# Layer 0's inner product as seven block products, a planner that prefers banks already taken, the gated update split between VectorE and GpSimd, and eps as a bias

## The chip, the cores and the metric

The kernel runs on one core of a Trainium2 chip. The metric is device time in microseconds (us). The kernel before took 1354.72 us (median of three runs, 1353.41 to 1354.8). The profile below is of one more execution, which took 1352.22 us; its span, from the first to the last instruction, is 1350.3 us.

The engines are named as in the profile: PE (TensorE, matrix products), PEld (its weight loads), DVE (VectorE), ACT (ScalarE), POOL (GpSimd), SP (SyncE, which issues nearly all DMAs).

## What is computed

The input is x, 64 graphs of 256 nodes with 128 channels, and one 256 x 256 adjacency matrix A, all float32. Four layers follow one another; each adds its result to its input and normalises over the channels.

```python
x = layernorm(x + sum_k (A^k x) W_k)        # layer 0: k = 0..3, W_k of both equal adjacency chains summed
x = layernorm(x + A (x W) + b)              # layer 1
x = layernorm(x + (D A+I D) x W^T + b)      # layer 2, D = degree^-1/2
# layer 3: five gated steps, then the residual and the norm
z  = sigmoid(av W3 + h U3 + b);  r = sigmoid(av W4 + h U3 + b)   # av = [A h, A h]
hv = tanh(av W5 + (r * h) U5 + b)
h  = (1 - z) * h + z * hv
```

Layer 0 is computed as x W0' + q W2' + A (x W1' + q W3') with q = A^2 x: W0' takes in the residual's identity, the others the sums of the two chains, all with their mean over the output channels taken out, so that the result is already centred and only its variance is left to find.

## The kernel before, in words

**Groups.** The 64 graphs are worked on as 32 groups of two. Two graphs times two node blocks make a tile of 128 x 512, the size of one PSUM bank. `record` (line 732) writes down the operations of one group, from its load through all four layers to its store. At most ten groups are under way at once (ACTIVE).

**The planner.** `Plan.add` (61) stores an operation with an engine, a cost in ns, a lag, a rank and what it reads and writes; `Plan.order` (84) then simulates the engines and writes out one fixed order for each. An operation whose output has no place yet needs a free slot of its kind (8 PSUM banks; numbers of SBUF tiles on line 203). Among the operations that could start, it takes the one with the earliest possible start, and at equal starts the one of the lowest rank, which is the older group (117). The engines run in that order, waiting on semaphores. The costs and ranks are used for nothing else.

**Propagation.** `seven` (593) forms A times a group's tile: [two graphs x two node blocks] times [2 x 2 blocks of A] with seven 128-wide block products in place of eight. GpSimd forms differences of input blocks (ts01, ts2, ts3; lines 613 to 621), PE forms the products in four operations: `first` (block 0, needs no difference), `middle` (three blocks), `more` (again into block 0, after ACT has copied it away as `kept`) and `rest`; DVE and ACT put the result m together (641 to 652).

**Layer 0** (lines 736 to 788). The transposed x (xT) is made by PE for the first two groups (`near`, HEAD = 4 graphs). For the other thirty a 32 x 32 block transpose on DVE (tx, 745), a DMA to DRAM and two DMAs back bring xT with its channels permuted; its weights are therefore a permuted copy w0p, made by four DMAs (306). After q has been propagated, `first` (764) makes, for each of two node blocks, four products of 256 columns: xT and q of each graph against two weight blocks side by side. ACT copies half of each bank to v, `second` multiplies v by A into the other half, and ACT copies that to s0.

**Norm.** `spread_of` (509): ACT squares the four parts of a tile and accumulates the sums; GpSimd adds eps (519) and raises to the power -1/2 (520). `normalise_centred` (526) then scales on ACT. This is used in layers 0 to 2 of every group and at the end of the last three.

**A gated step** (813 to 835). Four 512-wide products go into bank pr (w4 m and u3 hT for r, then w34 m on top for z), two into bank ph (w5 m, u5 rh). ACT turns pr to r, then, in place, to z; and ph, in place, to hv. DVE makes rh = r hT, d = hv - hT, e = z d (into pr), hT = hT + e. `packed` (699) then transposes blocks on DVE and brings h back in node order through DRAM by DMA. The last step of the last three groups (END = 6 graphs) goes to `closing` (557) instead.

**Head.** Weights and A are prepared in `pre` operations; `rows`, the transposes of ahat and `columns` (332 to 345) make layer 2's matrix.

Of the kernel before, what the change touches and what calls it, by code (L numbers as in the profile page):

```python
# [50 lines left out]
class Plan:  # L51
# [32 lines left out]
    def order(self):  # L84
# [14 lines left out]
        while any(ready.values()):  # L99
            best = None  # L100
            for e, waiting in ready.items():
                t0 = free.get(e, 0.0)
                pick = None
                for at, op in waiting:
                    need = {}
                    for v in placed[op]:
                        if v.slot is None:
                            need[v.kind] = need.get(v.kind, 0) + 1
                    short = False
                    for k, n in need.items():  # L110
                        if len(pool[k]) < n:
                            short = True
                            break
                        at = max(at, sorted(pool[k])[n - 1][0])
                    if short:
                        continue
                    key = (max(at, t0), op.rank, op.seq)
                    if pick is None or key < pick[0]:
                        pick = (key, op)
                if pick and (best is None or pick[0] < best[0]):  # L120
                    best = pick
            assert best, "the plan is stuck"
            (start, _, _), op = best
# [34 lines left out]
def kernel(  # L158
# [42 lines left out]
    SHAPES = {"bank": [P, 512], "x": [P, 512], "w": [P, 512], "th": [P, 384], "q": [P, P], "st": [P, Q * 6], "mv": [P, Q * 2],  # L201
              "ve": [P, Q], "rs": [P, Q]}
    slots = {"bank": BANKS, "x": ACTIVE + 3, "w": 48, "th": 10, "q": 10, "dram1": 8, "dram2": 16, "st": 12, "mv": 12, "ve": 24, "rs": 12}
# [31 lines left out]
    nc.vector.memset(half, -0.5)  # L235

# [67 lines left out]
    w0p = constant("w0p", [P, 2, C])  # L304

    def permuted():
        for r in range(4):
            nc.sync.dma_start(w0p.ap.rearrange("(j r) k c -> r j k c", r=4)[r], w0s.ap[32 * r:32 * (r + 1), 0:2, :])

    pre(1.2, "SP", 1800, permuted, [w0s], [w0p])  # L310
# [32 lines left out]
    pre(0.3, "DVE", 600, rows, [ahat, dinv], [ahat])  # L343
    pre(0.3, "PE", 4 * 110, lambda: turn(p_an, ahat), [ahat], [p_an])
# [64 lines left out]
    braw, bsum = constant("braw", [P, 6]), constant("bsum", [P, 3])  # L409
# [3 lines left out]
    pre(0.4, "DVE", 150, lambda: nc.vector.tensor_add(bsum.ap, braw.ap[:, :3], braw.ap[:, 3:]), [braw], [bsum])  # L413
    zb, rb, hb = ((bsum, bsum.ap[:, i:i + 1]) for i in range(3))
# [25 lines left out]
    class Group:  # L440
# [68 lines left out]
        def spread_of(self, tag, s):  # L509

            y, ve, rs = self.val("w", "y" + tag), self.val("ve", "ve" + tag), self.val("rs", "rs" + tag)

            def squares():
                for q in range(self.q):
                    nc.scalar.activation(nat(y)[:, q, :], nat(s)[:, q, :], AF.Square, scale=C ** -0.5,  # L515
                                         accum_out=ve.ap[:, q:q + 1])

            def scales():
                nc.gpsimd.tensor_scalar(ve.ap, ve.ap, EPS, None, op0=OP.add)  # L519
                nc.gpsimd.tensor_tensor(rs.ap, ve.ap, half[:, :self.q], op=OP.pow)  # L520

            self.act(squares, [s], [y, ve], 295 * self.q)
            self.add("POOL", 1330, 100, scales, [ve], [ve, rs])
            return y, rs
# [21 lines left out]
        def normalise(self, tag, s, mv, rs):  # L546
# [8 lines left out]
            return y  # L555

# [36 lines left out]
        def seven(self, tag, h, aTs, ins, blocks):  # L593
# [32 lines left out]
            def first():  # L626
                block(0, ins(h)[:, 0, 0], aTs.ap[:, 0, :P], True)

            def middle():
                block(2, row(ts, 0), sums.ap[:, 0, :])  # L630
                block(1, row(ts, 1), sums.ap[:, 2, :])
                block(3, row(ts, 2), sums.ap[:, 1, :])
# [21 lines left out]
            started = self.pe(pe_cost(P, 1), first, [h, aTs], [ps])  # L654
            kept = self.act(lambda: nc.scalar.copy(row(u, 1), row(ps, 0)), [ps], [u], 165)
# [3 lines left out]
            self.pe(pe_cost(P, 3), middle, [ts, sums], [ps], True, (started,))  # L659
# [59 lines left out]
        def gate_(self, name, ps, func, bias, kept=True):  # L719

            t = self.val("w", name) if kept else ps
            self.act(lambda: nc.scalar.activation(t.ap, ps.ap, func, bias=bias[1], scale=1.0),  # L722
# [9 lines left out]
        def record(self):  # L732
# [5 lines left out]
            if near:  # L738
                xT, w01 = self.copied("xT", self.transposes("x", x_)), w0s
            else:  # L740

                w01 = w0p
                turn, far = self.val("w", "tx"), self.val("dram", "dx")
                xT = self.val("w", "xT")
                self.dve(lambda: nc.vector.transpose(  # L745
                    turn.ap.rearrange("p (r b i t) -> p r b t i", r=4, t=T, i=32),
                    x_.ap.rearrange("p (b t r j) -> p r b t j", r=4, t=T, j=32)), [x_], [turn])
# [9 lines left out]
            v, s0 = self.val("w", "v"), self.val("w", "s0")  # L757
            py = []

            for t in range(T):  # L760
                p = self.val("bank", f"py0{t}")
                py.append(p)

                def first(p=p, t=t):
                    for b in range(self.nb):
                        o = p.ap[:, b * 2 * C:(b + 1) * 2 * C]
                        mm(o, (tiles if near else pairs)(xT)[:, b, t], w01.ap[:, 0:2, :], b == 0, True, shared=True)
                        mm(o, tiles(qT)[:, b, t], w0s.ap[:, 2:4, :], False, True, shared=True)

                def moved(p=p, t=t):  # L770
                    nc.scalar.copy(parts(v)[:, t], four(p)[:, :, 1, :])

                self.pe(pe_cost(2 * C, 2 * self.nb), first, [xT, qT, w01, w0s], [p])
                self.act(moved, [p], [v], 55 + 107 * self.nb)
            for t in range(T):

                def second(p=py[t], t=t):
                    for kt in range(T):
                        mm(four(p)[:, :, 0, :], aT.ap[:, kt, t * P:(t + 1) * P], parts(v)[:, kt],
                           False, True, shared=True)  # L780

                def summed(p=py[t], t=t):
                    nc.scalar.copy(nat(s0).rearrange("p (b t) c -> p t b c", t=T)[:, t],
                                          four(p)[:, :, 0, :])

                self.pe(pe_cost(self.nb * C, T), second, [v, aT], [py[t]])
                self.act(summed, [py[t]], [s0], 55 + 107 * self.nb)
# [25 lines left out]
            for s in range(STEPS):  # L813
# [10 lines left out]
                z = self.gate_(f"z{s}", pr, AF.Sigmoid, zb, False)  # L824
                self.product(ph, u5T, rh, False, True)
                hv = self.gate_(f"hv{s}", ph, AF.Tanh, hb, False)

                d = self.tensor(f"d{s}", OP.subtract, hv, hT)
                if s == STEPS - 1 and self.start >= B - END:
                    e = self.tensor("e", OP.mult, z, d, *self.by_tile)  # L830
                    break
                e = self.tensor(f"e{s}", OP.mult, z, d, into=pr)
                if s < STEPS - 1:
                    hT = self.tensor(f"hT{s}", OP.add, hT, e)
                    h, ats, ins = self.packed(f"h{s}", hT), aTp, pairs
            if self.start < B - END:
                hT = self.tensor("hT", OP.add, hT, e)
# [75 lines left out]
```

## Time and profile before

| | busy us | share of 1350.3 | what it does most |
|---|---|---|---|
| PE | 1336.5 | 99% | 512-wide products of the gated steps (810 us) |
| DVE | 940.9 | 70% | elementwise work of the steps |
| ACT | 758.1 | 56% | gates, squares, scaling |
| POOL | 680.7 | 50% | differences of blocks, powers, bias additions |
| DMA | | 34% of 16 engines | h and x through DRAM |

A group of instructions in the profile is written as line, engine, operation, output<-inputs, shapes and count, and then its busy time, the mean duration of one in ns, and the idle time of its engine before it with what ended that idle time. Each float32 product stands as two matmul records in the trace (160 products of ph<-rh are 320 records). A record of PE lasts longer than the distance to the next one, since matmuls overlap: 512-wide records last 593 ns and follow one another every 0.43 us. To find what a product costs PE, take the distance between starts and not the duration.

### The profile page before, as it was taken

How to read it: one execution, taken by the hardware profiler on the slowest of the kernel's cores; microseconds unless marked ns; L12 is line 12 of the kernel's file. 1: busy time of each engine (PE TensorE's matmuls, PEld its weight loads, DVE VectorE, ACT ScalarE, POOL GpSimd, SP SyncE). 2: the span in 40 equal slices, each digit the busy share in tenths (PEclk: the TensorE clock that was granted, in tenths of full speed). 3: DMA queues.
4: the chain of work that ended last, by engine and by line, in shares of the span. 5: the costliest groups of instructions: out<-in, count | busy, mean ns of one | idle time of the engine just before them, and what ended most of it. 6: DMA issues, size and time to landing. Idle time of an engine off the chain costs nothing.

```text
span 1350.3 us, 22012 instructions
## 1 busy us (share of the span) xinstructions
PE 1336.5 (99%) x6553; PEld 928.3 (69%) x6553; DVE 940.9 (70%) x2304; ACT 758.1 (56%) x2421; POOL 680.7 (50%) x1097
## 2 busy tenths in 40 slices
PE   8999999999999999999999999999999999999997
PEld 7886666676776766677666666676776776565554
DVE  5466677767667667865676776676666677877776
ACT  4675536467654556556565554474655686444445
POOL 5785425266742566247266443383653686233323
PEclk9999999999999999999999999999999999999999
DMA  6322334242522333333233433341332223333323
GB/s 175 109 71 71 94 94 128 77 128 78 147 78 77 111 95 118 115 106 100 64 110 110 127 100 98 94 137 56 110 102 63 82 85 121 87 106 95 93 78 110
DMA packets 269495, 134.96 MB, mean 100 GB/s; under 512 B 175776, under 2 KB 241056, under 8 KB 269376
## 3 DMA queue, kind: packets, MB, share of 16 engines
q1 hardware_dynamic: 269120, 133.42, 34.1%
q8 instruction: 53, 0.87, 0.3%
q14 instruction: 66, 0.54, 0.1%
q0 software_dynamic: 256, 0.13, 0.1%
HBM read 67.31 MB, written 65.80 MB: 99 GB/s over the span
## 4 chain that ended last, share of the span: by engine, by line
PE 95%; DVE 1%; DMA 1%; ACT 1%; issue 0%; SPq 0%; POOLq 0%; ACTq 0%; POOL 0%; DVEq 0%
PE pr L199 31%; PE ph L199 20%; PE pmg L199 19%; PE py L199 15%; PE pm L199 7%; PE pmq L199 3%; DMA x<-in_x_dram 1%; DMA w_raw<-in_L_gnn_weight_dram 0%; PE s L199 0%; DMA dx<-tx 0%; ACT y L515 0%; ACT y L551 0%; DVE s L543 0%; SPq L748 0%; DVE tx L745 0%
## 5 line engine op out<-in xcount | busy, mean ns | idle before, releaser
L199 PE MATMUL pr<-mg,w435u5T 128*128 128x512 f32 x640 | 319.8, 593 | 0.0
L614 POOL TENSOR_TENSOR tsg<-h 128x256 f32<-128x256 f32 x128 | 97.2, 760 | 292.5 <-DMA h<-dh 197.5
L722 ACT ACTIVATE r<-pr,bsum 128x512 f32<-128x512 f32 x160 | 109.7, 685 | 151.5 <-PE pr L199 150.7
L722 ACT ACTIVATE pr<-pr,bsum 128x512 f32<-128x512 f32 x160 | 105.5, 660 | 112.4 <-PE pr L199 109.3
L729 DVE TENSOR_TENSOR rh<-r,hT 128x512 f32<-128x512 f32 x160 | 122.7, 767 | 61.6 <-ACT r L722 60.7
L199 PE MATMUL ph<-rh,w435u5T 128*128 128x512 f32 x320 | 163.6, 594 | 0.0
L199 PE MATMUL ph<-mg,w435u5T 128*128 128x512 f32 x320 | 163.3, 592 | 0.0
L199 PE MATMUL pr<-hT,w2u3T 128*128 128x512 f32 x320 | 163.0, 593 | 0.0
L729 DVE TENSOR_TENSOR d<-ph,hT 128x512 f32<-128x512 f32 x160 | 109.7, 686 | 76.1 <-ACT ph L722 73.0
L199 PEld LDWEIGHTS pr<-mg,w435u5T 128*128 128x128 f32 x640 | 109.4, 191 | 65.3 <-issue 53.3
L722 ACT ACTIVATE ph<-ph,bsum 128x512 f32<-128x512 f32 x160 | 105.6, 660 | 60.4 <-PE ph L199 59.9
L531 ACT ACTIVATE y<-s,rs 128x128 f32<-128x128 f32 x384 | 122.1, 392 | 11.0 <-POOL rs L520 10.7
L515 ACT ACTIVATE y<-s 128x128 f32<-128x128 f32 x396 | 116.7, 299 | 16.9 <-DVE s L538 14.9
L199 PEld LDWEIGHTS pmg<-s_aTp,tsg 128*128 128x128 f32 x768 | 101.8, 192 | 33.5 <-issue 28.5
L652 DVE TENSOR_TENSOR mg<-pmg,usg 128x256 f32<-128x256 f32 x160 | 67.0, 419 | 72.7 <-PE pmg L199 70.4
L199 PEld LDWEIGHTS pmg<-aTp,h 128*128 128x128 f32 x512 | 87.1, 197 | 39.4 <-issue 29.2
L729 DVE TENSOR_TENSOR pr<-pr,d 128x512 f32<-128x512 f32 x157 | 108.7, 692 | 1.5
L520 POOL TENSOR_TENSOR rs<-ve,half 128x4 f32<-128x4 f32 x99 | 104.1, 1052 | 8.3
L519 POOL TENSOR_SCALAR ve<-ve 128x4 f32<-128x4 f32 x99 | 23.2, 234 | 166.6 <-ACT y L515 166.3
L729 DVE TENSOR_TENSOR hT<-hT,pr 128x512 f32<-128x512 f32 x157 | 106.1, 676 | 1.3
L199 PE MATMUL pmg<-s_aTp,tsg 128*128 128x128 f32 x768 | 106.2, 275 | 0.0
L642 DVE TENSOR_TENSOR usg<-usg,pmg 128x128 f32<-128x128 f32 x160 | 45.2, 284 | 81.7 <-PE pmg L199 47.7
(181 smaller groups left out, 2816.9 us busy)
## 6 DMA issues: line engine op xcount, KB each, us to landing
dh<-th SPq DMA_DIRECT2D x160, 256.0 KB, 2.0
h<-dh SPq DMA_DIRECT2D x256, 128.0 KB, 2.5
x<-in_x_dram SPq DMA_DIRECT2D x32, 256.0 KB, 3.4
hT<-dh SPq DMA_DIRECT2D x128, 64.0 KB, 2.0
out_dram<-y SPq DMA_DIRECT2D x32, 256.0 KB, 2.3
dx<-tx SPq DMA_DIRECT2D x30, 256.0 KB, 2.6
xT<-dx SPq DMA_DIRECT2D x60, 128.0 KB, 2.6
dn<-tn SPq DMA_DIRECT2D x29, 256.0 KB, 2.1
```

Source lines behind the costliest of these rows:

```text
L199: nc.tensor.matmul(o, lhsT, rhs, start=start, stop=stop, skip_group_check=shared)
L515: nc.scalar.activation(nat(y)[:, q, :], nat(s)[:, q, :], AF.Square, scale=C ** -0.5, accum_out=ve.ap[:, q:q + 1])
L519: nc.gpsimd.tensor_scalar(ve.ap, ve.ap, EPS, None, op0=OP.add)
L520: nc.gpsimd.tensor_tensor(rs.ap, ve.ap, half[:, :self.q], op=OP.pow)
L531: nc.scalar.mul(nat(y)[:, q, :], nat(s)[:, q, :], rs.ap[:, q:q + 1])
L614: nc.gpsimd.tensor_tensor(ts.ap[:, :2 * P].rearrange("p (x c) -> p x c", x=2), ins(h)[:, 1], ins(h)[:, :, 0], op=OP.subtract)
L642: nc.vector.tensor_tensor(row(u, 0), row(u, 1), row(ps, 3), op=OP.add)
L652: nc.vector.tensor_tensor(o(m, slice(1, 3)), o(ps, slice(1, 3), False), both, op=OP.add)
L722: self.act(lambda: nc.scalar.activation(t.ap, ps.ap, func, bias=bias[1], scale=1.0), [ps, bias[0]], [t], act_cost(self.width) + 100)
L729: self.dve(lambda: nc.vector.tensor_tensor(out(t), way(a), way(b), op=op), [a, b], [t])
```

## The change

1. **Layer 0.** For the thirty far groups, `inner_seven` replaces the two `first` operations: [two node blocks x {xT, q}] times the 2 x 2 weight blocks, with seven block products of two 128-column matmuls each. DVE forms four block sums (sd, ss, se, sf) of inputs and five of results; ACT copies one intermediate (u1) and half of s0. Sums of weights (w0t) are made by DVE; w0p and its DMAs go, and the block transpose tx reads x in another pattern that leaves the channels in order. The first two groups keep the old form (`inner`).
2. **Planner.** Of operations with equal start, those that open no new bank, and touch one that is taken, come ahead of all others; then the rank decides.
3. **Propagation.** `first` and `middle` become one operation, `opening`, behind GpSimd's differences.
4. **Gated step.** h = z hv + (1 - z) h: ACT makes a third gate, 1 - z = sigmoid(-pr), GpSimd multiplies it by hT (`stay`), z goes to SBUF, DVE makes z hv (into ph) and adds `stay`. d goes. The last step of the last three groups keeps the old form.
5. **eps.** A bias `root` = sqrt(eps/C) inside the squares in place of GpSimd's addition of eps.
6. **Head.** `rows` waits for w0s, and it and the transposes of ahat have later ranks.

```diff
-                    key = (max(at, t0), op.rank, op.seq)
+                    key = (max(at, t0), opens, op.rank, op.seq)
...
                     nc.scalar.activation(nat(y)[:, q, :], nat(s)[:, q, :], AF.Square, scale=C ** -0.5,
-                                         accum_out=ve.ap[:, q:q + 1])
+                                         bias=root[:, 0:1], accum_out=ve.ap[:, q:q + 1])
...
-                nc.gpsimd.tensor_scalar(ve.ap, ve.ap, EPS, None, op0=OP.add)
...
+            def times(o, a, w, start=False):
+                for b in range(NB):
+                    mm(o[:, b], a[:, b], w, start and b == 0, True, shared=True)
...
+            self.pe(pe_cost(P, NB), lambda: times(half(out_, 0), at(xT, 0), w0s.ap[:, 0, :], True), [xT, w0s], [out_])
+            self.act(lambda: nc.scalar.copy(u1.ap, out_.ap[:, :N]), [out_], [u1], 270)
+            self.pe(pe_cost(P, 2 * NB), both, [ss, st_, w0t], [more])
+            self.pe(pe_cost(P, NB), lambda: times(half(out_, 0), at(qT, 0), w0s.ap[:, 2, :]), [qT, w0s], [out_])
+            self.pe(pe_cost(P, NB), lambda: times(half(out_, 1), at(qT, 1), w0t.ap[:, 3, :]), [qT, w0t], [out_])
+            add(lambda: (u2.ap, u1.ap, more.ap[:, :N]), [u1, more], [u2])
+            self.pe(pe_cost(P, NB), lambda: times(half(more, 0), whole(sd), w0t.ap[:, 2, :]), [sd, w0t], [more])
+            add(lambda: (u3.ap, u1.ap, more.ap[:, :N]), [u1, more], [u3])
+            add(lambda: (half(v, 1), whole(u3), half(more, 1)), [u3, more], [v])
+            self.pe(pe_cost(P, NB), lambda: times(half(more, 1), whole(sf), w0s.ap[:, 3, :]), [sf, w0s], [more])
+            add(lambda: (half(v, 0), whole(u2), half(more, 1)), [u2, more], [v], True)
...
-            started = self.pe(pe_cost(P, 1), first, [h, aTs], [ps])
...
-            self.pe(pe_cost(P, 3), middle, [ts, sums], [ps], True, (started,))
+            self.pe(pe_cost(P, 4), opening, [h, ts, aTs, sums], [ps])
...
-                d = self.tensor(f"d{s}", OP.subtract, hv, hT)
...
-                e = self.tensor(f"e{s}", OP.mult, z, d, into=pr)
-                if s < STEPS - 1:
-                    hT = self.tensor(f"hT{s}", OP.add, hT, e)
+                    stay = self.gate_(f"v{s}", pr, AF.Sigmoid, less_zb, True, -1.0)
+                    self.add("POOL", 40 + 650 * self.nb, 100, lambda stay=stay, hT=hT: nc.gpsimd.tensor_tensor(
+                        stay.ap, stay.ap, hT.ap, op=OP.mult), [stay, hT], [stay])
...
+                e = self.tensor(f"e{s}", OP.mult, z, hv, into=ph)
+                hT = self.tensor(f"hT{s}", OP.add, e, stay)
```

## The prediction

> **What bounds the kernel now.** I read the page first, busy times in its first part:
>
> ```profile
> PE 1336.5 (99%) x6553; PEld 928.3 (69%) x6553; DVE 940.9 (70%) x2304; ACT 758.1 (56%) x2421; POOL 680.7 (50%) x1097
> ```
>
> PE is never idle on the average, the others have 30% or more to spare. An average can hide stages, so the busy times of three stages (columns: stretch, its length, then PE, PEld, DVE, ACT, POOL busy with counts, clock, DMA share, GB/s):
>
> ```profile
> 0.00:50.00 50.00, 44.76 (x256) 40.03 (x257) 26.89 (x78) 24.25 (x94) 29.81 (x54) 1.00 0.67 186
> 50.00:1330.00 1280.00, 1278.33 (x6236) 879.80 (x6235) 903.01 (x2194) 722.85 (x2289) 644.20 (x1034) 1.00 0.33 97
> 1330.00:1350.30 20.30, 13.40 (x64) 8.50 (x62) 10.95 (x33) 11.04 (x41) 6.72 (x10) 0.96 0.33 92
> ```
>
> Between 50 and 1330 us PE is idle for 1.7 us in all. So in the middle only two things count: how many PE nanoseconds are queued, and whether a new wait opens a gap. The head has 5.2 us of gaps, the tail some 7. The chain that ended last says the same (PE 95%). The waits of PE, longest in total first, show how few there are:
>
> ```profile
> PE warm L247 <- POOL ident masks.py:199: 1.4, 1, 1.4
> PE pmq L199 <- ACT mq L664: 1.3, 1, 1.3
> PE p_an L259 <- DVE ahat L334: 1.2, 1, 1.2
> PE pm L199 <- DVE m L648: 1.0, 2, 0.7
> PE py L199 <- DVE m L652: 0.6, 1, 0.6
> ```
>
> **What the Trainium skill says.** (1) "ScalarE: Activation LUTs", section "What ACT_TABLE_LOAD costs": an activation with immediate scale and bias has a fixed part, and each per-partition pointer operand adds about 93 ns. The trace agrees: at 128 x 128, the squares without a pointer (L515) take 299 ns, scaling by rs (L531) 392, scale and bias (L551) 484. (2) "SBUF — State Buffer", section "Who interferes with whom": a DVE instruction with two SBUF inputs and a GpSimd one that reads SBUF exclude each other; with one input from PSUM they don't. The trace agrees in direction: rh (r and hT in SBUF) takes 692 ns in the median, 767 in the mean, 1631 at most; d (one input in PSUM) 690, 686 and 694.
>
> **The change part by part.**
>
> *Layer 0 on PE.* I need the distance between starts. In the timeline of PE (start, length, instruction, count):
>
> ```profile
> 606.60 0.60 PE L199 MATMUL py<-w0p,xT 128*128 128x256 f32 x2
> 607.04 0.59 PE L199 MATMUL py<-w0s,mq 128*128 128x256 f32 x2
> 607.47 0.59 PE L199 MATMUL py<-w0p,xT 128*128 128x256 f32 x2
> 607.90 0.59 PE L199 MATMUL py<-w0s,mq 128*128 128x256 f32 x2
> 608.34 1.05 PE L199 MATMUL py<-w2u3T,m 128*128 128x128 f32 x8
> 609.23 0.81 PE L199 MATMUL py<-v,aT 128*128 128x256 f32 x3
> ```
>
> Four 256-wide products take 608.34 - 606.60 = 1.74 us; the two `first` of a group 3.47 us. Four 128-wide ones take 609.23 - 608.34 = 0.89, so fourteen 3.12; weights read with a step of two elements (xT, in 2 of the 14) cost about 6 ns more a record, as pmg<-aTp,h shows against pmg<-s_aTp,tsg: 4 records, 0.02. Gain 0.32 us a group, times 30: **-9.6 us**, range -9 to -10.5 by the rounding of the timeline. That there are 14 weight loads in place of 8 costs nothing: a load takes 190 ns beside products and the 128-wide rate above already has one for each record. `second` has the same four 256-wide products. All this is on the path, since PE has no gaps there.
>
> *Layer 0 elsewhere.* DVE gets 9 sums of 128 x 256 at 416 ns (L652) a group: +112 us; ACT loses 120 copies and gains 60 of 370 ns: -22; tx, 699 ns now, costs between that and, if the new read pattern is slower, the 1000 ns that the plan books: 0 to +9 us. SP loses four issues (2.4 us at 13 us), before which no xT waits. No one of these engines is the bound; priced at nothing but for the waits below.
>
> *Gated step,* 157 times. DVE loses d: 157 x 686 = -108 us, so it stays at about 950. ACT gains a gate of 660 ns: +104. POOL gains 128 x 512 products; nearest row, yb (128 x 512 on POOL, L795): 1289 ns, +202 us, less the 23 of the eps addition: 860 us or 64%. Nothing of it is on PE. The path from hv to h loses one DVE operation of 0.69, and gains a second arm, gate 0.66 and POOL 1.29 plus whatever stands in POOL's queue; it runs beside z, ph<-rh and hv (0.66 + 0.86 + 0.66).
>
> *eps.* The squares get a pointer: 392 - 299 = 93 ns, 396 times, +37 us of ACT; ACT comes to 758 + 104 - 22 + 37 = 877 us, 65%. For one norm: +4 x 93 = 0.37, minus POOL's L519 with its gap, 0.31: +0.06 us, hidden by other groups. In the tail it isn't: from 1340.8 ACT runs squares (1.14), a normalise (1.53), the last squares (1.2), then POOL, DVE, DMA. Two squares on that chain and one addition less: 2 x 0.37 - 0.31 = **+0.4 us**.
>
> *Head.* The built order moves p_an (waited 1.2 us for ahat) behind layer 0 of the first groups, but puts the transposes of raw_w and raw_u ahead of q. raw_u is issued at 6.4 us and takes 3.5 to 4.8 to land: 9.9 to 11.2. With 0.44 for those transposes q starts at 10.3 to 11.6, against 11.1 now; the work moved is alike. **-0.2 us**, -0.8 to +0.5. The later gaps of the head (some 3 us) may shrink or, with DVE's longer chain for layer 0, grow: -2 to +3, taken as 0.
>
> *New waits of PE in the middle.* The trace can't show them. Three sources. `opening` now waits for POOL, and behind it on PE stand other groups' products. rh meets POOL's new reads: blocked time now is 160 x (767 - 692) = 12 us, of which PE saw under 1 us as gaps; with reads on POOL up by some 40% and longer, 25 us, so 2 us. Products follow their inputs more closely: in the built order the PE work between the last sf product and `second` is 1.8 us in the median and 0.45 at least, against 0.16 (product's end) + 0.42 (sum) + semaphores; between u3's product and ph<-rh the least is 2.16 us in both kernels, against 1.75. Lower bound 0; upper bound 8 us, 50 ns for each of 160 steps. I take **+2.5 us**. Below nothing is excluded, as only 1.7 us of gaps are there to win. Dropping `kept`'s early start costs nothing: pmg's copy is hidden by other groups now, too.
>
> Sum: -9.6 + 0.4 - 0.2 + 2.5 = **-6.9 us**, a span of 1343.4. The profiled execution took 1352.22 against a median of 1354.72, so the difference is set against the median: **1347.8 us**.
>
> **The rivals.**
>
> *A: the planner's tight order eats the gain.* A rule that continues taken banks picks operations that have just become ready; every delay then reaches PE. For it: ACT's squares are booked at 295 ns each and will take more than before. Against it: booked lags (190 to 260 ns) exceed the semaphore gaps seen, about 60. At 50 ns for each of 160 steps: -9.6 + 0.4 - 0.2 + 8 = -1.4, **1353.3 us**.
>
> *B: POOL becomes the path (slower).* POOL is in order; a 1.29 us product ahead of ts01, ts2, ts3 (0.76 + 0.53 + 0.51) delays `opening`, which now holds block 0 as well. If an opening waits 90 ns on the average over the 157 steps, that is 14 us: -9.4 + 14 = +4.6, **1359.3 us**. It decides from 60 ns a step (9.4 us). Against it: 64% booked, and the longest stretch with PE idle now is 1.4 us.
>
> *C: the order closes the gaps too.* Head -2, no new waits: -9.6 + 0.4 - 2.2 = -11.4, **1343.3 us**. For it: banks held for a shorter time; against: hardly a gap to close in the middle.
>
> *D: no effect,* if the matmul records of 128 columns ran slower beside DVE's sums; the mixed stretches shown above speak against it. Counted in A.
>
> **How the numbers follow.** Forecast 0.62, A 0.18, B 0.10, C 0.10. A run of this kernel tells 0.2% (2.7 us) from no change. Forecast and C are faster; of A, half; B is slower, with a small part of A: faster 0.80, same 0.10, slower 0.10. Range: 1342.5 (C with its head) to 1353.5 (A); B and the far ends are left out.
>
> **What would show it.** PE's records: +12 x 30 = 360, with py/pz in 128-wide records at 0.11 us. Squares at 390 ns; POOL about 860 us with `stay` at 1.29; DVE about 950, rh's mean above 767. The windows: PE idle of 2 to 5 us between 50 us and the tail. Wrong if PE's waits name POOL's ts or `stay` for more than 5 us (B), or DVE and ACT in many small gaps (A), or if the 128-wide records come at more than 0.115 us.

## The result, and the profile after

The changed kernel takes **1360.03 us** (median of four runs, 1358.72 to 1360.58) against 1354.76 for the kernel before on the same chip: a ratio of 1.0040, interval [1.0022, 1.0057]. It is slower by some 5 us, where 7 us less were forecast. The profiled execution took 1359.85 us, with a span of 1358.1. All times in this document are of executions at nearly the full granted clock; the one profile of the run same_order fell in an execution at 0.654 of it (1981.44 us), so of that trace no duration is used.

Busy times of the whole span, from the page of the changed kernel:

```profile
PE 1334.2 (98%) x6913; PEld 931.4 (69%) x6913; DVE 988.2 (73%) x2423; ACT 854.5 (63%) x2518; POOL 861.2 (63%) x1155
```

and in the three stages of the prediction (columns as there):

```profile
0.00:50.00 50.00, 41.91 (x254) 37.81 (x255) 36.26 (x95) 18.74 (x63) 26.54 (x45) 0.97 0.53 137
50.00:1330.00 1280.00, 1271.08 (x6564) 880.16 (x6564) 935.48 (x2277) 820.64 (x2408) 827.31 (x1101) 1.00 0.34 98
1330.00:1358.10 28.10, 21.23 (x99) 13.40 (x97) 16.45 (x52) 15.12 (x48) 7.39 (x11) 0.95 0.32 95
```

PE has 360 more records, as forecast. But between 50 and 1330 us it now stands idle for 1280.00 - 1271.08 = 8.9 us, where it was 1.7. The waits of PE, longest in total first:

```profile
PE ptx L783 <- DMA x<-in_x_dram: 3.1, 1, 3.1
PE pmg L201 <- ACT usg L768: 2.2, 4, 1.0
PE pmq L201 <- DVE mq L758: 2.1, 2, 1.6
PE pmg L201 <- DVE mg L758: 1.5, 1, 1.5
PE p_w2u3T L408 <- DMA raw_u<-in_L_gnn_u_w_dram: 1.4, 1, 1.4
PE warm L252 <- POOL ident masks.py:199: 1.4, 1, 1.4
PE ph L201 <- DVE rh L838: 1.2, 4, 0.4
```

The lines of the head (ptx, p_w2u3T, warm, and 1.6 us of pmq) are DMA and start-up. In the others no single culprit stands out: between 50 and 1330 us VectorE and ScalarE end small waits before many kinds of product, about 4 us each, and GpSimd ends none.

Idle time undercounts, because a record of PE lasts longer than the distance to the next. A finer measure takes from the trace the distance between the starts of neighbouring matmul records, and counts as a **gap** what exceeds 112, 216 or 429 ns (for 128, 256 and 512 columns) by more than 30 ns. Between 50 and 1330 us the kernel before has 5.6 us of gaps, in both of its profiles, and the changed one 19.0. At those unhindered distances all products together (4155, 792 and 1606 records of the three widths before; 4995, 312 and 1606 after) take 1325.4 us before and 1315.8 after: **the change saves 9.6 us of PE's work and loses more than that in time without a product.**

The comparison with the span needs care. A second profile of the kernel before (run before_again) has a span of 1353.4, not 1350.3: the first product of layer 0 started at 17.85 us there and at 14.57 in the first one. Of these 3.3 us, 1.7 come from the weights (VectorE first used w_raw at 10.14 us against 8.43, and the product that PE waits for in the head stands behind it) and 1.6 from the granted clock, which stood at half for 3.4 us. The first profile of the kernel before has no such stretch in its head; that of the changed kernel has one. Here are the stretch of before_again, that of the changed kernel, and one of about the same length from the first profile (columns as before, the clock third from the end):

```profile
11.86:15.27 3.41, 3.41 (x13) 2.93 (x14) 3.31 (x11) 0.58 (x1) 0.00 (x0) 0.50 0.39 95
13.58:17.00 3.42, 2.87 (x8) 2.33 (x9) 3.32 (x13) 0.37 (x1) 0.00 (x0) 0.50 0.56 156
11.11:14.57 3.46, 3.46 (x18) 3.05 (x17) 3.42 (x13) 1.17 (x2) 0.00 (x0) 1.00 0.60 170
```

So the second profile is the fairer one to compare with. Measured against it, time outside products (the span less the products at their unhindered distances) grows by 1.4 us up to 20 us, by 2.3 from 20 to 100, by 10.6 from 100 to 1330, and not at all after that. Together 14.3 - 9.6 = +4.7, and the spans differ by 1358.1 - 1353.4 = 4.7.

What did VectorE's new work cost? Its groups, shapes kept apart (output<-inputs, count, then busy us, mean ns of one, idle before):

```profile
L852 DVE STREAM_TRANSPOSE tx<-x 128x512 f32<-128x512 f32 x30 | 33.4, 1114 | 4.2 <-DMA x<-in_x_dram 4.2
L645 DVE TENSOR_TENSOR u<-u,pz 128x256 f32<-128x256 f32 x60 | 24.7, 413 | 5.5 <-PE pz L201 5.3
L623 DVE TENSOR_TENSOR se<-ss,xT 128x256 f32<-128x256 f32 x30 | 19.7, 662 | 0.3
L620 DVE TENSOR_TENSOR ss<-xT,mq 128x256 f32<-128x256 f32 x30 | 19.7, 661 | 0.2
L626 DVE TENSOR_TENSOR sf<-mq,se 128x256 f32<-128x256 f32 x30 | 18.8, 632 | 0.4
L617 DVE TENSOR_TENSOR sd<-xT 128x256 f32<-128x256 f32 x30 | 17.1, 571 | 1.0 <-DMA xT<-dx 1.0
```

The additions with a PSUM input (u<-u,pz) take 413 ns, close to the 416 that the prediction gave to all nine sums. The four sums whose two inputs both lie in SBUF take 571 to 662 ns, one and a half times as long. And the code books all of them in the planner at 340.

One of the longer stalls shows what that does. The timeline of the changed kernel (start, length, engine, instruction, count, idle before):

```profile
269.32 1.54 DVE L620 TENSOR_TENSOR ss<-xT,mq 128x256 f32<-128x256 f32 x2
...
270.79 1.83 DVE L623 TENSOR_TENSOR se<-ss,xT 128x256 f32<-128x256 f32 x2
...
270.91 1.42 POOL L906 TENSOR_TENSOR v<-v,hT 128x512 f32<-128x512 f32 x1 [0.33 <-ACT v L831]
...
272.54 1.55 DVE L626 TENSOR_TENSOR sf<-mq,se 128x256 f32<-128x256 f32 x2
...
272.82 1.06 PE L201 MATMUL py<-w2u3T,m 128*128 128x128 f32 x8
...
274.01 0.27 DVE L752 TENSOR_TENSOR usg<-usg,pmg 128x128 f32<-128x128 f32 x1
274.32 0.29 DVE L755 TENSOR_TENSOR wsg<-usg,pmg 128x128 f32<-128x128 f32 x1
...
275.00 0.29 DVE L758 TENSOR_TENSOR mg<-wsg,pmg 128x128 f32<-128x128 f32 x1 [0.39 <-ACT mg L773]
...
275.34 0.50 PE L201 MATMUL pmg<-s_aTp,h 128*128 128x128 f32 x2 [1.46 <-DVE mg L758]
```

Six sums run from 269.32 to 274.09, 4.8 us where 6 x 340 = 2.0 were booked. Behind them in VectorE's fixed order stand usg, wsg and mg of another group (ScalarE's copy that mg needs had itself waited for wsg), and PE's next product waits 1.46 us for that mg, though VectorE is busy for only 73% of the span.

### The profile page after: what moved, and what is told of

Same layout as the page of the kernel before. It is cut to its first block, busy times and chain, and to the rows that moved or that the text cites. A ratio compares the mean times of both kernels' runs of the same rounds, so it can differ in the third digit from the quotient of the medians.

```text
span 1358.1 us, 22918 instructions
## 1 busy us (share of the span) xinstructions
PE 1334.2 (98%) x6913; PEld 931.4 (69%) x6913; DVE 988.2 (73%) x2423; ACT 854.5 (63%) x2518; POOL 861.2 (63%) x1155
## 4 chain that ended last, share of the span: by engine, by line
PE 73%; DVE 3%; ACT 2%; issue 1%; DMA 1%; POOLq 0%; POOL 0%; SPq 0%; DVEq 0%; ACTq 0%
PE pr L201 25%; PE ph L201 17%; PE pmg L201 15%; PE py L201 7%; PE pm L201 5%; PE pz L201 3%; PE pmq L201 2%; ACT y L525 1%; DVE rh L838 0%; PE s L201 0%; ACT y L540 0%; DVE ss L620 0%; ACT y L560 0%; DMA xT<-dx 0%; DVE sd L617 0%
## 5 line engine op out<-in xcount | busy, mean ns | idle before, releaser
L906 POOL TENSOR_TENSOR v<-v,hT 128x512 f32<-128x512 f32 x157 | 203.0, 1293 | 225.2 <-ACT v L831 215.5
L201 PE MATMUL pr<-mg,w435u5T 128*128 128x512 f32 x640 | 324.0, 594 | 0.5 <-DVE mg L762 0.2
L831 ACT ACTIVATE v<-pr,bsum 128x512 f32<-128x512 f32 x157 | 107.5, 685 | 120.1 <-PE pr L201 119.8
L525 ACT ACTIVATE y<-s,root 128x128 f32<-128x128 f32 x396 | 153.8, 392 | 20.5 <-DVE s L547 19.2
L838 DVE TENSOR_TENSOR ph<-z,ph 128x512 f32<-128x512 f32 x157 | 108.0, 690 | 68.4 <-ACT ph L831 67.7
L201 PEld LDWEIGHTS pmg<-aTp,h 128*128 128x128 f32 x512 | 91.7, 196 | 71.3 <-issue 43.9
L540 ACT ACTIVATE y<-s,rs 128x128 f32<-128x128 f32 x384 | 122.4, 395 | 10.9 <-POOL rs L529 10.3
L838 DVE TENSOR_TENSOR hT<-ph,v 128x512 f32<-128x512 f32 x157 | 107.0, 684 | 6.3 <-POOL v L906 0.8
L831 ACT ACTIVATE z<-pr,bsum 128x512 f32<-128x512 f32 x157 | 107.1, 682 | 0.0
L872 POOL TENSOR_TENSOR yb<-y,wb 128x512 f32<-128x512 f32 x64 | 82.6, 1290 | 31.5 <-ACT y L540 31.0
L201 PE MATMUL pmg<-aTp,h 128*128 128x128 f32 x512 | 99.7, 280 | 1.3 <-ACT usg L768 1.2
```

The source lines that it names most:

```text
L201: nc.tensor.matmul(o, lhsT, rhs, start=start, stop=stop, skip_group_check=shared)
L540: nc.scalar.mul(nat(y)[:, q, :], nat(s)[:, q, :], rs.ap[:, q:q + 1])
L838: self.dve(lambda: nc.vector.tensor_tensor(out(t), way(a), way(b), op=op), [a, b], [t])
L872: nc.gpsimd.tensor_tensor(nat(yb), nat(y), bias[1][:, None, :].to_broadcast([P, self.q, C]), op=OP.add)
L906: self.add("POOL", 40 + 650 * self.nb, 100, lambda stay=stay, hT=hT: nc.gpsimd.tensor_tensor(stay.ap, stay.ap, hT.ap, op=OP.mult), [stay, ...
```

## The experiments

Theory (T): VectorE's new work takes longer than it is booked for, the sums above all because they collide with GpSimd's reads; in a fixed order with PE full, that lateness becomes gaps. Rivals: a single other part of the change costs the time (the gated step with its GpSimd product, the preference for taken banks, the head), or the new layer 0 has too few free banks whatever its sums take. All times below are medians of several executions, beside the kernel before in the same session. The kernel before itself lies between 1354.07 and 1355.06 us in these sessions. In the profiles of no_l0, no_head, stay_dve and booked_490 the granted clock stood at half for 3.4 us somewhere between 1097 and 1125 us, in that of copies_others for 6.8 us; without the records in these stretches the gaps are the figures in brackets.

| run | time | before | ratio, interval | gaps 50 to 1330 |
|---|---|---|---|---|
| no_l0 | 1358.01 | 1354.07 | 1.0034 [1.0023, 1.0046] | 9.6 (7.9) |
| no_step | 1356.28 | 1354.07 | 1.0020 [1.0011, 1.0029] | 12.4 |
| no_plan | 1364.01 | 1354.07 | 1.0084 [1.0070, 1.0098] | 21.3 |
| no_head | 1359.56 | 1354.07 | 1.0043 [1.0032, 1.0055] | 21.5 (19.9) |
| only_plan | 1357.64 | 1354.57 | 1.0023 [1.0013, 1.0032] | 6.5 |
| stay_dve | 1359.03 | 1354.57 | 1.0035 [1.0022, 1.0047] | 16.4 (14.8) |
| psum_sums | 1347.75 | 1354.57 | 0.9951 [0.9938, 0.9963] | 8.2 |
| same_order | 1357.08 | 1354.79 | 1.0016 [1.0010, 1.0023] | |
| doubled | 1378.30 | 1354.79 | 1.0173 [1.0157, 1.0190] | 33.7 |
| booked | 1347.61 | 1354.79 | 0.9950 [0.9936, 0.9963] | 8.7 |
| copies | 1359.38 | 1354.79 | 1.0036 [1.0024, 1.0049] | 18.6 |
| booked_490 | 1360.84 | 1355.06 | 1.0041 [1.0028, 1.0053] | 21.6 (19.9) |
| booked_900 | 1349.43 | 1355.06 | 0.9958 [0.9944, 0.9971] | 10.5 |
| others | 1353.38 | 1355.06 | 0.9989 [0.9983, 0.9996] | 12.7 |
| booked_all | 1343.97 | 1355.06 | 0.9918 [0.9904, 0.9931] | 5.5 |
| copies_others | 1356.00 | 1354.61 | 1.0008 [1.0000, 1.0017] | 16.6 (12.9) |
| booked_all_no_step | 1348.13 | 1354.61 | 0.9950 [0.9937, 0.9962] | 8.0 |

### One part of the change taken back: no_l0, no_step, no_plan, no_head

Each is the changed kernel with one part as it was. no_l0 has the old `first` and w0p (part 1 of the change undone), no_step the old gated step (part 4 undone). The other two:

```diff
no_plan
-                    key = (max(at, t0), opens, op.rank, op.seq)
+                    key = (max(at, t0), op.rank, op.seq)
no_head
-    pre(0.9, "DVE", 600, rows, [ahat, dinv, w0s], [ahat])
-    pre(1.1, "PE", 4 * 110, lambda: turn(p_an, ahat), [ahat], [p_an])
+    pre(0.3, "DVE", 600, rows, [ahat, dinv], [ahat])
+    pre(0.3, "PE", 4 * 110, lambda: turn(p_an, ahat), [ahat], [p_an])
```

> The changed kernel with layer 0 as before (two 256-wide first operations, permuted weights, the old block transpose), all else as changed. PE gets its 9.6 us of work back. Theory 1 (DVE's block sums with two SBUF inputs and GpSimd's reads hold each other up, and the delays reach PE): the gaps of PE between 50 and 1330 us, 19 us in the changed kernel against 5.6 before, fall to 8 or less, so 1357 to 1359 us. Theory 2 (the order that continues taken banks is too tight, whatever the work): gaps stay at 15 to 19, 1366 to 1369 us.

> The changed kernel with the gated step as before (d, z d, h + z d on DVE; no third gate, no product on GpSimd). GpSimd falls from 861 to about 660 us busy. Theory 1 (sums and GpSimd's reads hold each other up): the gaps of PE in the middle fall from 19 to 8 to 11 us and the block sums from 570 to 660 ns to below 550, 1350 to 1353 us. Theory 2 (tight order): gaps stay at 15 to 19, 1357 to 1361 us.

> The changed kernel without the preference for taken banks; all else as changed. Theory 2 (tight order): the gaps of PE in the middle fall from 19 to 7 to 10 us, 1349 to 1352 us. Theory 1: gaps stay at 15 us or more, 1356 to 1362 us.

> The changed kernel with the ranks and waits of the preparation of layer 2's matrix as before. Theory 3 (the new order of the head costs the 5 us by which layer 0's first product starts later, 19.1 us against 14.6): it starts before 16 us, and the time falls by 3 to 5 us to 1355 to 1357. If the later start came from transfers that landed late in that one execution: no change beyond 2 us, 1358 to 1362.

Measured: 1358.01, 1356.28, 1364.01 and 1359.56. No single removal brings the kernel back to 1354. Without the new layer 0 the gaps fall to 9.6 us (7.9), near what T expected, but the saving of 9.6 us of PE goes with them, and the time moves by 2 only. no_step falls between its two expectations: the sums still take 562 to 614 ns, the gaps are 12.4 us, the time is some 3 to 4 us better. The head does nothing that can be told. The preference for banks *helps* the changed kernel by some 4 us, where the rival wanted its removal to help. But each of these edits reorders every engine, so an effect and a reshuffled order can't be told apart in them. That is why the next runs hold the order fixed.

### The bank rule alone, and GpSimd's product moved: only_plan, stay_dve

```diff
only_plan (on the kernel before)
-                    key = (max(at, t0), op.rank, op.seq)
+                    key = (max(at, t0), opens, op.rank, op.seq)
stay_dve (on the changed kernel)
-                    stay = self.gate_(f"v{s}", pr, AF.Sigmoid, less_zb, True, -1.0)
-                    self.add("POOL", 40 + 650 * self.nb, 100, lambda stay=stay, hT=hT: nc.gpsimd.tensor_tensor(
-                        stay.ap, stay.ap, hT.ap, op=OP.mult), [stay, hT], [stay])
...
+                    stay = self.tensor(f"v{s}", OP.mult, self.gate_(f"v{s}", pr, AF.Sigmoid, less_zb, False, -1.0), hT)
```

> The kernel before with the preference for taken banks and nothing else of the change. Inside the changed kernel the preference was worth 4.5 us. If that carries over: 1349 to 1351 us. Theory 2 (it makes the order tight): gaps of PE in the middle rise from 5.6 us to 8 or more, 1357 to 1360 us.

> The changed kernel with (1 - z) h made by DVE from PSUM: z goes to SBUF first, 1 - z overwrites pr in place, DVE multiplies it by hT. ACT keeps its third gate, GpSimd loses the product (861 to about 660 us), DVE gains 157 of 690 ns (988 to about 1090). If GpSimd's product is what cost 3.2 us of the gated step: as with the old step, 1355 to 1357 us. If the third gate on ACT is: 1359 us or more, gaps as in the changed kernel.

The bank rule on the old kernel costs 3 us (1.0023), though its gaps in the middle are only 1 us longer (6.5); in the changed kernel it was worth some 4. Its sign depends on what it orders. Moving the 1.29 us product from GpSimd to VectorE (POOL 861 to 667 us busy, DVE 988 to 1059) leaves 1359.03: with GpSimd relieved of 194 us the time stays, which speaks against GpSimd's queue as the path, the slower rival of the prediction. It isn't a clean test, since VectorE gets 71 us more. The run's other expectation, that ScalarE's third gate is what costs, fits the time; no run takes that gate away alone.

### The collisions taken away in one order: psum_sums, same_order, doubled

In psum_sums the product of x's first block comes first and each sum reads its result from PSUM as one of its inputs, so layer 0 computes something else; the instructions, their number and their bookings stay. same_order is the same program with the inputs in SBUF again; the two traces show the same order of instructions on every engine. doubled is psum_sums with each sum executed twice and booked once.

```diff
psum_sums
-                nc.vector.tensor_tensor(whole(ss), at(xT, 1), at(qT, 1), op=OP.add)
+                nc.vector.tensor_tensor(whole(ss), half(out_, 0), at(qT, 1), op=OP.add)
...
-            self.add("DVE", 340, 260, s1, [xT, qT], [ss])
+            self.add("DVE", 340, 260, s1, [xT, qT, out_], [ss])
same_order (on psum_sums)
-                nc.vector.tensor_tensor(whole(ss), half(out_, 0), at(qT, 1), op=OP.add)
+                nc.vector.tensor_tensor(whole(ss), at(xT, 1), at(qT, 1), op=OP.add)
doubled (on psum_sums)
+                for _ in range(2):
+                    nc.vector.tensor_tensor(whole(ss), half(out_, 0), at(qT, 1), op=OP.add)
```

> The changed kernel, with one input of each of layer 0's four block sums taken from the bank of the first product in PSUM in place of x or q in SBUF (so layer 0 computes something else, with as many instructions and one more wait of the sums for that product). No sum has two SBUF inputs. Theory 1 (sums and GpSimd's reads hold each other up, and that is what reaches PE): the sums fall from 570 to 660 ns to about 415, the gaps of PE between 50 and 1330 us from 19 to 10 to 13 us, the time by 5 us or more to at most 1354. Theory 4 (it is the longer chain of layer 0 on an engine with more work, tx at 1114 ns included, not the collisions): the sums get shorter all the same, the gaps stay at 16 us or more and the time at 1357 to 1362.

> The order on every engine is that of the kernel with sums from PSUM (psum_sums, 1347.75 us), instruction for instruction; only the operands of the four sums are x and q in SBUF again, as in the changed kernel, so that the result is the reference's. Theory 1 (two SBUF inputs against GpSimd's reads): the sums are back at 570 to 660 ns, the gaps of PE in the middle at 15 us or more, the time at 1356 to 1361 us. If psum_sums was fast because its order happened to be a good one: 1347 to 1350 us.

> psum_sums (inputs from PSUM, layer 0 computes something else) with each sum done twice in the same place, which the planner is not told: DVE is busy 50 us longer than there, twice what the collisions add to the sums in the changed kernel (some 26 us), without a second SBUF input. If it is the unbooked time on DVE that reaches PE, collision or not: 12 us or more lost, 1360 us or more. If what hurts is that sums and GpSimd's operations hold each other up in turn: less than 6 us lost, at most 1354 us.

The sums of psum_sums, in the groups of VectorE:

```profile
L617 DVE TENSOR_TENSOR sd<-py,xT 128x256 f32<-128x256 f32 x30 | 12.6, 420 | 3.2 <-ACT u L648 2.0 <-PE py L201 0.9
L620 DVE TENSOR_TENSOR ss<-py,mq 128x256 f32<-128x256 f32 x30 | 12.4, 416 | 0.6 <-ACT u L648 0.5
L623 DVE TENSOR_TENSOR se<-py,xT 128x256 f32<-128x256 f32 x30 | 12.3, 413 | 0.2 <-ACT u L648 0.2
L626 DVE TENSOR_TENSOR sf<-mq,py 128x256 f32<-128x256 f32 x30 | 12.3, 409 | 0.0
```

All four are back at 409 to 420 ns, with GpSimd as busy as ever (818 us between 50 and 1330, against 827). In the changed kernel's trace the 20 sums with no GpSimd work beside them take 415 ns on average, 24 with half to nearly all of their time beside it 675, and 69 with all of it 699; in psum_sums all four classes lie between 413 and 415. That ties the excess to an instruction of GpSimd at work at the same time and to both inputs being in SBUF. It is what the Trainium skill, "SBUF — State Buffer", section "Who interferes with whom", states, with a price for this shape that the runs add. The rival of too few free banks finds no support: psum_sums uses the same two banks a group, fills one of them earlier, and is fast.

In one and the same order, the SBUF inputs cost 1357.08 - 1347.75 = **9.3 us** (9.1 when each is taken against the kernel before of its own session). Taken at the changed kernel's means, the sums then last (571 + 661 + 662 + 632) / 4 = 632 ns instead of 415, or 217 x 120 = 26 us more of VectorE. Doubling the sums adds 120 x 415 = 50 us of VectorE and costs 30.6 us. So every microsecond of unbooked VectorE work cost, as an estimate, 0.36 us in the one case and 0.61 in the other, though VectorE is idle for over a quarter of the span (busy 71% in psum_sums, 73% in doubled). A collision holds up GpSimd too (861 us busy in the changed kernel, 850 in psum_sums); how much of the 9.3 us comes by that way isn't separated.

### The same work, booked: booked, booked_490, booked_900

```diff
-            self.add("DVE", 340, 260, s3, [xT], [sd])
-            self.add("DVE", 340, 260, s1, [xT, qT], [ss])
-            self.add("DVE", 340, 260, s2, [xT, ss], [st_])
-            self.add("DVE", 340, 260, s4, [qT, st_], [sf])
+            self.add("DVE", 640, 260, s3, [xT], [sd])
+            self.add("DVE", 640, 260, s1, [xT, qT], [ss])
+            self.add("DVE", 640, 260, s2, [xT, ss], [st_])
+            self.add("DVE", 640, 260, s4, [qT, st_], [sf])
```

(490 and 900 in place of 640 in the other two.)

> The changed kernel with the sums booked at 640 ns in place of 340, near what they take there; nothing else. If the loss comes from the plan not knowing of the time: the gaps of PE in the middle fall from 19 to 12 us or less, the time to at most 1354 us. If the collisions fall at random and a longer mean does not help an in-order queue: 1356 to 1361 us.

> The changed kernel with the sums booked at 490 ns, half way between 340 and 640. If the loss follows the unbooked time: between the two, gaps of PE in the middle 11 to 16 us, 1350 to 1356 us. If orders are good or bad by chance: anything from 1347 to 1364.

> The changed kernel with the sums booked at 900 ns, well above the 560 to 670 they take. If what matters is that the plan books no less than is taken: as booked, 1346 to 1350 us, gaps 7 to 11 us. If chance: anything from 1347 to 1364.

With 640 the sums still take 562 to 671 ns, so hardly any of the work is gone, and the kernel takes 1347.61: 12 us won by telling the planner. 900 is nearly as good (1349.43). But 490 wins nothing (1360.84, gaps 21.6, or 19.9). That is a miss for T in its simple form, which wanted something between 1360 and 1347. It leaves two readings: that a booking helps only from near what is taken, or that each booking draws another order and orders differ by chance. The runs don't decide between them here; each number was tried in one order only.

### The rest of the new work booked: others, booked_all

The remaining new or slower instructions were booked at what the trace of the changed kernel has: the 256-wide additions at 415 (from 340), tx at 1114 (from 1000), and the squares, which now carry a pointer for their bias, at 390 (from 295).

```diff
-                self.dve(lambda: nc.vector.tensor_tensor(*parts_(), op=OP.add), reads, writes, 340, joint)
+                self.dve(lambda: nc.vector.tensor_tensor(*parts_(), op=OP.add), reads, writes, 415, joint)
...
-                     x_.ap.rearrange("p (b t j r) -> p r b t j", r=4, t=T, j=32)), [x_], [turn], 1000)
+                     x_.ap.rearrange("p (b t j r) -> p r b t j", r=4, t=T, j=32)), [x_], [turn], 1114)
...
-            self.act(squares, [s], [y, ve], 295 * self.q)
+            self.act(squares, [s], [y, ve], 390 * self.q)
```

booked_all has these and the sums at 640.

> The changed kernel with the sums left at 340 ns, but the other new operations booked at what they take: the five 256-wide additions 415 in place of 340, tx 1114 in place of 1000, the squares with the bias 390 each in place of 295. If every unbooked time counts alike (30 x 5 x 75 ns, 30 x 114 ns and 396 x 95 ns, together 52 us on two engines, more than the sums' 35): 1352 us or less. If it is the sums: 1356 to 1361 us.

> Both: the sums at 640 ns and the other new operations at what they take. If the plan's truth is what counts: at least as fast as booked, 1344 to 1348 us. If chance: anything from 1347 to 1364.

others alone wins 6.7 us over the changed kernel, between its two expectations; booked_all wins 16: 1343.97 us, **0.8% faster than the kernel before** (0.9918 [0.9904, 0.9931]). Its middle stage, and two of its sums:

```profile
50.00:1330.00 1280.00, 1278.35 (x6608) 887.69 (x6607) 946.97 (x2322) 827.75 (x2427) 829.30 (x1102) 1.00 0.34 98
```

```profile
L617 DVE TENSOR_TENSOR sd<-xT 128x256 f32<-128x256 f32 x30 | 20.6, 688 | 1.8 <-DMA xT<-dx 1.8
L620 DVE TENSOR_TENSOR ss<-xT,mq 128x256 f32<-128x256 f32 x30 | 19.9, 662 | 0.2
```

PE is idle for 1.7 us between 50 and 1330, exactly as in the kernel before, and its gaps are 5.5 us. The sums are no shorter than in the changed kernel. VectorE's longer work is still there; PE no longer waits for it.

The pair of squares that the bias concerns, as ScalarE's timeline of the changed kernel shows them:

```profile
1122.07 0.41 ACT L525 ACTIVATE y<-s,root 128x128 f32<-128x128 f32 x1
1122.37 0.20 ACT L525 ACTIVATION_READ_ACCUMULATOR y<-s,root 128x1 f32 x1
1122.46 0.40 ACT L525 ACTIVATE y<-s,root 128x128 f32<-128x128 f32 x1
```

They follow one another every 0.39 us; in the kernel before it was 0.30 (1105.76, 1106.05, 1106.34), which is what was booked.

### A remedy that failed: copies, copies_others

ScalarE copies the second block of xT, and q, into the PSUM bank that the group is about to use, so that each sum has one input in PSUM and the result stays right. The sums are booked at 420, the copies at 370 and 600. copies_others adds the bookings of `others`.

```diff
-            self.add("DVE", 340, 260, s1, [xT, qT], [ss])
+            self.act(lambda: nc.scalar.copy(half(more, 0), at(xT, 1)), [xT], [more], 370)
+            self.act(q_copy, [qT], [more], 600)
+            self.add("DVE", 420, 260, s1, [xT, more], [ss])
...
-                nc.vector.tensor_tensor(whole(ss), at(xT, 1), at(qT, 1), op=OP.add)
+                nc.vector.tensor_tensor(whole(ss), half(more, 1), at(xT, 1), op=OP.add)
```

> The changed kernel with a remedy that keeps the result: ACT copies one block of xT and then q into the bank that is free until the products need it (256 and 512 columns a group, 30 us of ACT in all), and the sums are formed as xT0 - xT1, q1 + xT1, q1 - sd, q0 - se, each with one input from PSUM. Theory 1: the sums take about 415 ns, the gaps in the middle are 8 to 11 us, the time is 1347 to 1350 us, faster than both kernels. If the bank that is held longer or ACT's copies cost as much as the collisions: 1354 us or more.

> The kernel with ScalarE's two copies into PSUM, and with the other new work (256-wide adds, transposes of x, squares) booked at what it measured. Theory (the copies failed because the rest of the new work was still unbooked, so that ScalarE and VectorE came late whatever the sums took): sums stay near 415 ns, gaps of PE at most 9 us between 50 and 1330 us, time 1343 to 1349 us, as the version that books everything. Rival (the PSUM bank that the copies hold, or ScalarE's two extra instructions in the chain of a group, cost as much as the collisions did): 1353 us or more, gaps 12 us or more.

The sums do fall to 410 to 418 ns in both. The times are 1359.38 and 1356.00, with gaps of 18.6 and 16.6 us (12.9 outside the stretch of half clock). So the remaining unbooked work was not the whole reason: the rival holds, and the way to the sums through a bank and through ScalarE costs about as much as the collisions. Which of the two, the bank held from the copies on (one of eight) or ScalarE's two instructions in front of each group, isn't separated.

### The gated step in an order that fits: booked_all_no_step

booked_all with part 4 of the change undone.

> The version that books all new work, with the gated step of before (h by d and zd on VectorE, gate copies as before). If the split of h over GpSimd is worth something once the order is right: 1347 us or more (VectorE about 1053 us busy instead of 986). If the split costs, as leaving it out of the changed kernel had it (1356.28 against about 1360): 1342 us or less. If it is neutral: 1343 to 1346 us.

1348.13 against 1343.97: here the split of h over GpSimd is worth 4 us, where in the changed kernel it seemed to cost 3 to 4 (no_step). The same edit has two signs under two orders. It takes 75 us from VectorE (1060.6 without it, 985.9 with it); that this is why it pays here is likely, but not shown.

Taken together: the four kernels whose plan books the sums at 640 or more (booked, booked_900, booked_all, booked_all_no_step) take 1343.97 to 1349.43 us; the eight whose sums have both inputs in SBUF and are booked at 340 or 490 (the changed kernel, no_step, no_plan, no_head, stay_dve, same_order, booked_490, others) take 1353.38 to 1364.01. With four kernels on one side and eight on the other, chance alone is an unlikely account, though it isn't excluded for any single pair.

### The kernel before once more: before_again

> The kernel before, once more, for a second profile of its head. If the later landing of the weights (w_raw used at 10.9 us in the changed kernel, 8.4 before) is a matter of the execution: layer 0's first product starts between 15 and 19 us here too, and the time at 20 us not spent on products is 6 to 10 us. If it is the change's: 14.6 us and 5.6 us as before.

1355.34 us, span 1353.4, gaps 5.6. So the later start of layer 0 is mostly a matter of the execution. The figures for the head above rest on both profiles.

## Why the prediction was wrong

**The work of PE** was right: -9.6 us were forecast for the 128-wide products, and the products at their unhindered distances make -9.6. The 360 records came.

**The busy times** were nearly right where the row was right: POOL 861 (860), `stay` 1293 ns (1289), the squares 392 ns (392), ACT 854 (877). DVE is 988 and not 950.

**The step that failed** is the term "New waits of PE in the middle", taken at +2.5 us with an upper bound of 8 us. The runs put some 13 us in its place (10.6 after 100 us, 2.3 between 20 and 100). Of its three sources, `opening` waiting for POOL can't be seen in PE's waits, and the collisions of rh, which were to double and cost 2 us, hardly grew:

```profile
L838 DVE TENSOR_TENSOR rh<-r,hT 128x512 f32<-128x512 f32 x160 | 123.2, 770 | 46.2 <-ACT r L831 45.3
```

The mean was 767 before. The third source, products that follow their inputs more closely, is nearest to what came, but it looked at the additions behind the products and not at the four sums ahead of them. The term failed in two places that lead to it.

First, its sizes. The line "9 sums of 128 x 256 at 416 ns (L652)" took a row whose addition has one input in PSUM, and applied it to four sums that have both in SBUF. The page of the skill was quoted in the prediction for exactly that difference, but only for rh. The row rh, which has both inputs in SBUF, was there to take. The mean over the four sums is 632 ns, 26 us more of VectorE than priced; tx takes 1114 ns and not at most 1000.

Second, its weight. This extra VectorE time was "priced at nothing but for the waits below", since VectorE has 30% to spare. Spare time on the average doesn't hide lateness in an engine that runs a fixed order: the pair psum_sums and same_order shows 9.3 us for the sums' excess alone, and doubled, in the order of psum_sums, 30.6 for 50 us more. What counts, as booked and booked_all point to, is less the duration than the difference between it and what was booked, 632 against 340; booked_490 doesn't fit that simply. The prediction weighed this for the squares alone (rival A: "booked at 295 ns each and will take more").

**Rival A**, the planner's tight order, named the right mechanism, delays that reach PE, and its sign, many small gaps of DVE and ACT, is what the waits show. It gave them 8 us, for a time of 1353.3; with 13 it would have been 1358. Its stated cause, the preference for taken banks, isn't borne out: without it the changed kernel is slower still. **Rival B**, GpSimd as the path, came nearest with its number, 1359.3, but by luck: PE waits for no POOL instruction in the middle, and stay_dve changes little. That booked_all comes to **C**'s number (1343.97 against 1343.3) is luck too, since it needed other bookings. **D** fell with the first point.

**The head** was put at -0.2 us. Time outside products up to 20 us is 1.4 us longer than in before_again, 4.7 longer than in the first profile, in whose head the clock never fell; but no_head doesn't change the time. The start of q was misread: 10.3 to 11.6 us were forecast, and it started at 14.40 (13.3 in others), right behind the transpose that had waited for raw_u; in before_again, without that wait, it started at 13.54. **eps in the tail** (+0.4) wasn't tried alone, nor was the merged `opening`. After 1330 us the time outside products is 7.0 us in the changed kernel and 7.1 in before_again, so of the +0.4 nothing can be seen; a small part of `opening` isn't excluded.

What stays open: how much of the difference between two orders is chance. That 490 does no better than 340, and that a part changes sign between orders, suggests that a single reorder can be worth 3 to 5 us either way. The forecast's range had no term for it. What doesn't hang on that are the runs in one order (9.3 and 30.6 us).

## What to carry to other kernels

Where a planner turns booked durations into a fixed order, a new instruction has two prices, its duration and its error in the booking; with the bounding engine full, the second can be the larger. So before an edit is priced as hidden, compare each new booking with the nearest row of the *same operand placement* (both inputs in SBUF, or one in PSUM), take its mean and not its lone duration, and book that. After a change to the work, book again from the new trace before judging any of its parts: here that turned +0.4% into -0.8%.

## What the runs showed of the hardware

- A 128 x 256 addition on VectorE with both inputs in SBUF takes 415 ns alone and about 700 beside GpSimd's work, 1529 at most (changed kernel); with one input in PSUM it is 382 to 428 in all 120 cases (psum_sums).
- A block transpose of 128 x 512 on VectorE that reads x with a stride of four elements takes 1114 ns (changed kernel); with the old pattern, 32 neighbouring elements at a time, it took 699 (704 in no_l0).
- The granted clock of PE can fall to half for 3.41 us, or twice that, within an execution of normal length. In the head of the changed kernel the records of q that start in such a stretch follow one another every 427 ns, the later ones every 216; the 16 records took 4.74 us, against 3.46 in the first profile of the kernel before and in others, whose heads have no such stretch. Idle time before q doesn't by itself slow it: in others PE had waited 2.0 and 1.2 us and q still took 3.46. Those two profiles have the shortest idle stretches in the head (1.2 and 2.0 us at most, against 2.2 to 4.2 in the other seventeen at normal clock), so idle time may be what brings the stretch on; no run tests that, and some profiles have such a stretch near 1100 us with PE at work.
